# Preparing one quarter of the first batch alone before a recurrence starts

## The chip, the core and the metric

The kernel runs on one core of one Trainium2 chip. The metric is device microseconds of one execution. Five engines work side by side on the core: TensorE (PE in the profile), VectorE (DVE), ScalarE (ACT), GpSimd (POOL) and SyncE (SP, which here only issues transfers). They are joined by semaphores, which the tile framework inserts; each engine takes its own instructions strictly in the order in which they were put in its queue.

## The reference, cut to what matters

The input is `x` of 8 batches x 384 channels x 32 x 32 positions, fp32. Layer 0 is a bidirectional selective scan with a depthwise convolution beside it, layer 1 a causal attention and a quantised feed-forward net. For the change only layer 0 up to its recurrence matters:

```python
xn = rmsnorm(x)                                      # over the 384 channels
u, z = split(xn @ in_proj_w.T)
u = silu(causal_conv1d(u, 4 taps) + bias)            # fwd; on the flipped sequence for bwd
dt, Bm, Cm = split(u @ x_proj_w.T)                   # 24, 16, 16 rows
delta = softplus(dt @ dt_proj_w.T + dt_proj_b)       # [L, 384]
h = exp(delta * A) * h + (delta * u) * Bm            # over L = 1024 positions, 16 states a channel
y = sum(h * Cm, over the 16 states) + u * D
g = (y * silu(z)) @ out_proj_w.T                     # fwd + bwd
x = x + 0.5 * (0.25 * g + sigmoid(depthwise3x3(xn)) * xn)
# layer 1: t = t + attention(layernorm(t)); t = t + bitlinear_ffn(layernorm(t))
```

## The kernel before, in words

Channels lie on the 128 partitions in three chunks `c`, positions along the free axis in two halves `h` of 512. The two directions `d` and two halves make four quarters of a batch, which the recurrence takes in the order `PARTS = ((0,0),(0,1),(1,1),(1,0))` (direction, half): forward first half, forward second half, and then backward from the far end.

**The recurrence** is cut into `Unit`s: a quarter has 24 (3 chunks x 4 groups of 4 states x 2), a batch 96, the kernel 768. One unit is: on POOL one multiply `g = ud * B` (`s_first`, L612), on ACT two exponentials `da` (L625), on DVE two scans of 512 steps (L633), on ACT, in the quarters that open a direction, a copy of the carry (L638), on POOL a second multiply `g * C` (`s_scan`, L639), and on PE four matmuls that sum the states (`s_sum`, L652). `ud` (delta times u) and `dl` (delta) are read from DRAM, each row spread over four partitions (`s_load`, for the unit `AHEAD + 2` = 4 slots on); B and C come from the DRAM tile `rows` (`s_row`).

**The preparation** of a batch is `before_scan`: load `x`, normalise each half (L343), `in_proj` (three matmuls on PE, copy on ACT L359), `conv` (for the first batch a scale on ACT L369, three multiply-adds on DVE L380, bias on ACT L390; for later batches matmuls with diagonal taps), `silus` (L445, between two loads of the activation table), `sum_of_us` (L449), stores of `u` to DRAM, `project` (`xd`, L499 on PE, L510 on ACT, L512 on DVE), the store of the B and C rows (L520), and `delta` (L532 to L548: one matmul, six ACT and four DVE instructions of 128x512, a load of `u` from DRAM and two stores, `sud` and `sdl`). `gates` makes the silu of z and the local 3x3 convolution (L411, on DVE).

**The order.** Each stage is a list of steps with a guessed weight in us (`Steps`; 2.5 if none is given), and `run(a, b)` interleaves lists in proportion to the weights. The batch that comes first has its whole preparation put into the list `begin`, run alone; only its z and `gates` are in `beside`. Then 102 slots of the recurrence (`first`) run with `beside`: the z and gates of batch 0, the whole preparation of batches 1, 2 and 3, and `binarize` of both feed-forward weights. After that attention and feed-forward of batch after batch are interleaved with the remaining units. That order gives each instruction its priority: the framework schedules by a timing model, and an engine with nothing ready of high priority is given later work. So `binarize` stands in `beside` but runs in part during `begin`.

Loads and stores are issued by SP (`load`, L117; `spill`, L130), the constants and `binarize`'s transfers by ACT. Of the tile pools, `big` has 6 buffers of 128x3072 (a batch's `xn`, the diagonal `taps`, pieces of the binarised weights), `mid` has 10 of 128x1024; eight banks of PSUM are shared by tags.

Of the kernel before, what the change touches and what calls it, by code (L numbers as in the profile page):

```python
# [58 lines left out]
def kernel(  # L59
# [258 lines left out]
    def before_scan(b, tags, emit, later=None, diags=None):  # L318
# [8 lines left out]
        @emit  # L327
        def _():

            st["xn"] = btile(f"xn_{b}")  # L330
            load(st["xn"], x[b].rearrange("(c p) l -> p c l", p=P))
            st["xd"] = mtile(f"xd_{b}")

        for h in range(NH):

            @emit
# [78 lines left out]

        def weights_of(c):
# [8 lines left out]
        emit(lambda: weights_of(0))  # L425
        for c in range(NC):

            @emit
            def _(c=c):
                st["up", c] = mtile(f"up_{b}_{c}")  # L430
                for d in range(2):
                    st["u", d, c] = mtile(f"u{d}_{b}_{c}")
                if c + 1 < NC:
                    weights_of(c + 1)

            for i, to in enumerate((emit, emit if later is None else later)):
                for h in range(NH):
                    to(lambda c=c, i=i, h=h: in_proj(c, i, h), 2.6)
            for d in range(2):
                for h in range(NH):  # L440
                    emit(lambda c=c, d=d, h=h: conv(c, d, h), 3.0)
# [5 lines left out]
            def sum_of_us(c=c):  # L447
# [3 lines left out]
                for d in range(2):  # L451
                    spill((b, "u", d, c), st["u", d, c], f"su_{d}_{b}_{c}")
# [27 lines left out]
            def gates_of_us(c=c, silus=silus, sum_of_us=sum_of_us):  # L480
                with tc.high_priority(offset=60):
                    silus([st["u", 0, c], st["u", 1, c]])
# [10 lines left out]
            for h in range(NH):  # L493

                def project(c=c, h=h):
                    xp = bank_of(f"xp_{b}_{c}_{h}")
                    for d in range(2):
                        with at_once(d == 1):
                            mm = nc.tensor.matmul(  # L499
                                out=xp[d * DW : (d + 1) * DW, :],  # L500
                                lhsT=wx[:, c, :],
                                rhs=st["u", d, c][:, half(h)],
                                start=True,
                                stop=True,
                            )
                        if d == 1:
                            pin(mm)
                    xd = st["xd"][:, half(h)]
                    if c == 0:
                        nc.scalar.activation(xd, xp, AF.Identity, bias=onerow)  # L510
                    else:
                        nc.vector.tensor_tensor(xd, xd, xp, ALU.add)  # L512

                emit(project)

        @emit
        def _():
            for d in range(2):
# [724 lines left out]
```

## Time and profile before

| | |
|---|---|
| median of 3 runs | 4453.81 us (4451.62 to 4459.21) |
| profiled execution | 4445.17 us, span 4443.4 us |
| busy: PE, DVE, ACT, POOL | 83%, 76%, 63%, 81% of the span |
| first instruction of the recurrence on POOL | starts at 142.53 us |
| last one ends | 4209.8 us |
| units of the recurrence | 768, of two POOL instructions of 2.37 us each |

The profiled execution lies 8.6 us under the median of the three runs. Busy time is the time in which an engine executes; waiting, issuing of transfers and semaphores are not counted. An L-number is a line of the kernel above.

### The profile page before, as it was taken

How to read it: one execution, taken by the hardware profiler on the slowest of the kernel's cores; microseconds unless marked ns; L12 is line 12 of the kernel's file. 1: busy time of each engine (PE TensorE's matmuls, PEld its weight loads, DVE VectorE, ACT ScalarE, POOL GpSimd, SP SyncE). 2: the span in 40 equal slices, each digit the busy share in tenths (PEclk: the TensorE clock that was granted, in tenths of full speed). 3: DMA queues.
4: the chain of work that ended last, by engine and by line, in shares of the span. 5: the costliest groups of instructions: out<-in, count | busy, mean ns of one | idle time of the engine just before them, and what ended most of it. 6: DMA issues, size and time to landing. Idle time of an engine off the chain costs nothing.

```text
span 4443.4 us, 43447 instructions
## 1 busy us (share of the span) xinstructions
PE 3701.6 (83%) x12522; PEld 1421.4 (32%) x12522; DVE 3385.8 (76%) x4707; ACT 2803.9 (63%) x5383; POOL 3588.3 (81%) x1560
## 2 busy tenths in 40 slices
PE   3587786998889988889988799988999956997799
PEld 1132222333323333233332233322333312332244
DVE  6899999678977789877798867988676766667623
ACT  4767778576764767756677666776665733664334
POOL 0678889888888898799888998889989899889700
PEclk7696887989988999888998899988899877898899
DMA  6645555224363334642344623446332242224200
GB/s 214 242 150 199 189 206 205 102 98 148 123 228 116 102 126 148 208 160 100 110 137 163 212 98 109 154 148 228 103 105 95 78 146 99 95 83 146 84 18 29
DMA packets 327240, 612.01 MB, mean 138 GB/s; under 512 B 33321, under 2 KB 92121, under 8 KB 327001
## 3 DMA queue, kind: packets, MB, share of 16 engines
q1 hardware_dynamic: 317344, 593.09, 38.7%
q10 hardware_dynamic: 9656, 16.15, 1.1%
q8 instruction: 98, 1.61, 0.1%
q14 instruction: 142, 1.16, 0.1%
HBM read 443.45 MB, written 165.68 MB: 137 GB/s over the span
## 4 chain that ended last, share of the span: by engine, by line
PE 49%; DVE 27%; ACT 9%; issue 6%; POOL 5%; DMA 4%; SPq 0%; ACTq 0%; DVEq 0%; POOLq 0%
DVE g L633 13%; PE s L800 8%; PE pt L883 5%; PE qp L740 5%; PE yp L1052 5%; PE av L897 5%; PE y L652 5%; PE op L710 3%; PE in L352 2%; POOL g L612 2%; PE hp L1008 2%; POOL g L639 2%; DVE loc L411 2%; DVE u L380 2%; ACT da L625 2%
## 5 line engine op out<-in xcount | busy, mean ns | idle before, releaser
L612 POOL TENSOR_TENSOR g<-ud,bc 128x1024 f32<-128x1024 f32 x768 | 1820.1, 2370 | 401.8 <-DMA ud<-sud 145.5
L639 POOL TENSOR_TENSOR g<-g,bc 128x1024 f32<-128x1024 f32 x768 | 1816.8, 2366 | 212.8 <-ACT carry L638 113.4
L625 ACT ACTIVATE da<-dl,amat 128x512 f32<-128x512 f32 x1536 | 1054.8, 690 | 806.7 <-DVE g L633 794.1
L633 DVE TENSOR_TENSOR_SCAN g<-da,carry,g 128x512 f32<-128x512 f32 x768 | 942.8, 1267 | 216.4 <-POOL g L612 177.5
L633 DVE TENSOR_TENSOR_SCAN g<-da,g 128x512 f32<-128x512 f32 x768 | 897.9, 1207 | 154.0 <-POOL g L612 99.3
L652 PE MATMUL y<-g,gather 128*32 128x512 f32 x3072 | 470.4, 689 | 145.1 <-POOL g L639 125.3
L800 PE MATMUL s<-k,q 64*128 64x512 f32 (+3 forms) x1152 | 498.9, 618 | 67.9 <-DVE nm L813 65.4
L813 DVE CUSTOM_DVE_ANT_0 pr<-s,cmask 128x512 f32<-128x512 f32 (+3 forms) x576 | 306.2, 550 | 324.0 <-PE s L800 270.0
L1008 PE MATMUL hp<-t,w 128*128 128x512 f32 x720 | 345.7, 626 | 47.2 <-ACT h L1016 31.4
L886 ACT COPY ptn<-pt 128x512 f32<-128x512 f32 (+3 forms) x576 | 263.1, 477 | 187.2 <-PE pt L883 186.0
L1052 PE MATMUL yp<-h,w 128*128 128x512 f32 x720 | 335.5, 621 | 45.2 <-DVE h L1034 40.6
L883 PE MATMUL pt<-ident,pr 128*128 128x128 f32 x1728 | 337.4, 310 | 12.7 <-ACT ptn L886 11.3
L352 PE MATMUL in<-xn,win 128*128 128x512 f32 x576 | 290.6, 649 | 68.8 <-DVE xc L474 18.1
L883 PEld LDWEIGHTS pt<-ident,pr 128*128 128x128 f32 x1728 | 204.8, 151 | 381.2 <-ACT ptn L886 116.7
L411 DVE SCALAR_TENSOR_TENSOR loc<-xn,vec,loc 128x496 f32<-128x496 f32 (+3 forms) x384 | 265.7, 717 | 14.5 <-ACT loc L400 12.6
L833 ACT ACTIVATE pr<-pr,low 128x512 f32<-128x512 f32 (+3 forms) x384 | 241.3, 630 | 48.0 <-DVE low L827 43.7
L897 PE MATMUL av<-ptn,v 128*64 128x512 f32 (+3 forms) x1152 | 268.6, 532 | 2.2 <-ACT ptn L886 2.2
L532 PE MATMUL dp<-xd,wdt 25*128 25x512 f32 x192 | 157.6, 949 | 129.0 <-ACT du L545 105.9
L740 PE MATMUL qp<-t,wqk 128*128 128x512 f32 x576 | 253.6, 596 | 3.4 <-DVE t L313 3.4
L800 PEld LDWEIGHTS s<-k,q 64*128 64x128 f32 x1152 | 167.3, 213 | 265.2 <-DVE nm L813 160.9
L1008 PEld LDWEIGHTS hp<-t,w 128*128 128x128 f32 x720 | 137.3, 198 | 253.3 <-issue 150.9
L1052 PEld LDWEIGHTS yp<-h,w 128*128 128x128 f32 x720 | 139.3, 198 | 246.7 <-issue 181.3
(149 smaller groups left out, 4364.9 us busy)
## 6 DMA issues: line engine op xcount, KB each, us to landing
ud<-sud SPq DMA_DIRECT2D x384, 256.0 KB, 4.3
dl<-sdl SPq DMA_DIRECT2D x384, 256.0 KB, 3.3
bc<-rows SPq DMA_DIRECT2D x256, 256.0 KB, 3.8
t<-st SPq DMA_DIRECT2D x63, 512.0 KB, 6.2
su<-u SPq DMA_DIRECT2D x48, 512.0 KB, 2.9
du<-su SPq DMA_DIRECT2D x96, 256.0 KB, 4.5
sud<-du SPq DMA_DIRECT2D x96, 256.0 KB, 2.9
sdl<-du SPq DMA_DIRECT2D x96, 256.0 KB, 3.5
```

Source lines behind the costliest of these rows:

```text
L352: nc.tensor.matmul(out=mp, lhsT=st["win", c][:, k, i, :], rhs=st["xn"][:, k, half(h)], start=(k == 0), stop=(k == NC - 1),)
L612: pin(nc.gpsimd.tensor_tensor(g, ud, rows_for(u, 0), ALU.mult))
L625: nc.scalar.activation(da, sst["dl", u.b, u.c, u.part, u.q][:, i, :], AF.Exp, scale=amat[:, u.c, k, u.j : u.j + 1],)
L633: nc.vector.tensor_tensor_scan(gi[:, ::step], da[:, ::step], gi[:, ::step], first, ALU.mult, ALU.add)
L639: pin(nc.gpsimd.tensor_tensor(g, g, rows_for(u, 1), ALU.mult))
L652: mm = nc.tensor.matmul(out=y[k * BLK : (k + 1) * BLK, :], lhsT=gather, rhs=pair[k // 2][:, k % 2, :], start=(u.j == u.first_group), stop= ...
L740: nc.tensor.matmul(out=qp, lhsT=st["wqk"][:, c, o : o + P], rhs=st["xn"][:, c, half(h)], start=(c == 0), stop=(c == NC - 1),)
L800: mm = nc.tensor.matmul(out=ss[e][:, : k1 - k0], lhsT=st["q"][rows_of(e), c, chunk(qi)], rhs=st["k"][rows_of(e), c, k0:k1], start=True, st ...
L883: nc.tensor.transpose(pt[:, chunk(i)], pr[:, e, chunk(j % QT)], ident)
L897: mm = nc.tensor.matmul(out=av[rows_of(e), cols], lhsT=st["v"][:, j, hd * HD : (hd + 1) * HD], rhs=st["ptn", j, e][:, cols], start=(j == 0 ...
L1008: nc.tensor.matmul(out=hp, lhsT=st["w1"][:, c, chunk(m % 2)], rhs=st["xn"][:, c, half(h)], start=(c == 0), stop=(c == NC - 1),)
L1052: nc.tensor.matmul(out=yp, lhsT=st["w2", k // 6][:, k % 6, :], rhs=st["h", k // NC][:, k % NC, half(h)], start=(k == 0), stop=(k == NF - 1),)
```

## The change

For the first batch `before_scan` gets a third list of steps, `lead`. What leads up to the deltas of the quarter (direction 0, half 0) goes into it: the load of `x` (now in two transfers, one for each half), the norm of half 0, all three weight loads, `in_proj` and `conv` of that quarter for the three chunks, one group of three silus of 128x512, the store of these u's, their projection (rows of direction 0 alone), the store of their B and C rows, and three `delta` steps. `lead` is run alone. The other three quarters' steps go into `beside`, ahead of everything else that was there; the z and gates of batch 0 follow them (`more`), then the other batches as before. The first batch's `up` and forward `u` live in two `big` buffers in place of six `mid` ones. `project` becomes `project_parts`, which does one direction or both; u and row stores go half by half (`keep_u`, `keep_rows`).

```diff
@@ -315,7 +315,7 @@
                     )
 
 
-    def before_scan(b, tags, emit, later=None, diags=None):
+    def before_scan(b, tags, emit, later=None, diags=None, lead=None):
 
 
         st = {}
@@ -324,16 +324,23 @@
         def bank_of(name):
             return bank(name, next(turns))
 
-        @emit
+        at_half = (emit if lead is None else lead, emit)
+
+        @at_half[0]
         def _():
 
             st["xn"] = btile(f"xn_{b}")
-            load(st["xn"], x[b].rearrange("(c p) l -> p c l", p=P))
+            given = x[b].rearrange("(c p) l -> p c l", p=P)
+            if lead is None:
+                load(st["xn"], given)
+            else:
+                for h in range(NH):
+                    load(st["xn"][:, :, half(h)], given[:, :, half(h)])
             st["xd"] = mtile(f"xd_{b}")
 
         for h in range(NH):
 
-            @emit
+            @at_half[h]
             def _(h=h):
                 sqs = squares(st["xn"], h, f"n0_{b}")
                 ms = mean_of(lambda c: sqs[c], f"ms_{b}_{h}")
@@ -413,6 +420,43 @@
                 )
             return acc
 
+        def project_parts(c, h, parts):
+            xp = bank_of(f"xp_{b}_{c}_{h}_{len(parts)}_{parts[0]}")
+            for d in parts:
+                with at_once(d != parts[0]):
+                    mm = nc.tensor.matmul(
+                        out=xp[d * DW : (d + 1) * DW, :],
+                        lhsT=wx[:, c, :],
+                        rhs=st["u", d, c][:, half(h)],
+                        start=True,
+                        stop=True,
+                    )
+                if d != parts[0]:
+                    pin(mm)
+            rows = slice(parts[0] * DW, (parts[-1] + 1) * DW)
+            xd = st["xd"][rows, half(h)]
+            if c == 0:
+                nc.scalar.activation(xd, xp[rows, :], AF.Identity, bias=onerow[rows, :])
+            else:
+                nc.vector.tensor_tensor(xd, xd, xp[rows, :], ALU.add)
+
+        def keep_u(c, d, h):
+            if (b, "u", d, c) not in spilled:
+                spilled[b, "u", d, c] = dram.tile(
+                    [P, L], F32, name=f"su_{d}_{b}_{c}", tag=f"sp_u_{d}_{c}"
+                )
+            nc.sync.dma_start(out=spilled[b, "u", d, c][:, half(h)], in_=st["u", d, c][:, half(h)])
+
+        def keep_rows(d, h):
+            if (b, "rows", d) not in spilled:
+                spilled[b, "rows", d] = dram.tile(
+                    [2 * NS, L], F32, name=f"rows{d}_{b}", tag=f"rows{d}"
+                )
+            nc.sync.dma_start(
+                out=spilled[b, "rows", d][:, half(h)],
+                in_=st["xd"][d * DW + BC0 : (d + 1) * DW, half(h)],
+            )
+
         def weights_of(c):
             w = mtile(f"win_{b}_{c}", NC * 2 * P).rearrange("p (k i e) -> p k i e", k=NC, i=2)
             for i in range(2):
@@ -422,23 +466,53 @@
                 )
             st["win", c] = w
 
-        emit(lambda: weights_of(0))
+        at_half[0](lambda: weights_of(0))
+        if lead is not None:
+
+            @lead
+            def _():
+                ups, us = btile(f"ups_{b}"), btile(f"us0_{b}")
+                for c in range(NC):
+                    st["up", c], st["u", 0, c] = ups[:, c, :], us[:, c, :]
+                    if c > 0:
+                        weights_of(c)
+
+            for c in range(NC):
+                lead(lambda c=c: in_proj(c, 0, 0), 2.6)
+                lead(lambda c=c: conv(c, 0, 0), 3.0)
+
+            @lead
+            def _():
+                for c in range(NC):
+                    u = st["u", 0, c][:, half(0)]
+                    pin(nc.scalar.activation(u, u, AF.Silu))
+                pin(nc.scalar.preload_act_table_set(LOG_EXP))
+                for c in range(NC):
+                    keep_u(c, 0, 0)
+
+            for c in range(NC):
+                lead(lambda c=c: project_parts(c, 0, (0,)))
+            lead(lambda: keep_rows(0, 0))
+
         for c in range(NC):
 
             @emit
             def _(c=c):
-                st["up", c] = mtile(f"up_{b}_{c}")
-                for d in range(2):
+                if lead is None:
+                    st["up", c] = mtile(f"up_{b}_{c}")
+                for d in range(2) if lead is None else (1,):
                     st["u", d, c] = mtile(f"u{d}_{b}_{c}")
-                if c + 1 < NC:
+                if lead is None and c + 1 < NC:
                     weights_of(c + 1)
 
             for i, to in enumerate((emit, emit if later is None else later)):
                 for h in range(NH):
-                    to(lambda c=c, i=i, h=h: in_proj(c, i, h), 2.6)
+                    if lead is None or (i, h) != (0, 0):
+                        to(lambda c=c, i=i, h=h: in_proj(c, i, h), 2.6)
             for d in range(2):
                 for h in range(NH):
-                    emit(lambda c=c, d=d, h=h: conv(c, d, h), 3.0)
+                    if lead is None or (d, h) != (0, 0):
+                        emit(lambda c=c, d=d, h=h: conv(c, d, h), 3.0)
 
             def silus(ts):
                 for t in ts:
@@ -448,8 +522,12 @@
                 usum = mtile(f"us_{b}_{c}")
                 nc.vector.tensor_tensor(usum, st["u", 0, c], st["u", 1, c], ALU.add)
                 spill((b, "us", c), usum, f"sus_{b}_{c}")
-                for d in range(2):
-                    spill((b, "u", d, c), st["u", d, c], f"su_{d}_{b}_{c}")
+                if lead is None:
+                    for d in range(2):
+                        spill((b, "u", d, c), st["u", d, c], f"su_{d}_{b}_{c}")
+                else:
+                    for d, h in ((0, 1), (1, 1), (1, 0)):
+                        keep_u(c, d, h)
 
 
             def gates(c=c, silus=silus, sum_of_us=sum_of_us):
@@ -479,7 +557,7 @@
 
             def gates_of_us(c=c, silus=silus, sum_of_us=sum_of_us):
                 with tc.high_priority(offset=60):
-                    silus([st["u", 0, c], st["u", 1, c]])
+                    silus([st["u", 0, c] if lead is None else st["u", 0, c][:, half(1)], st["u", 1, c]])
                     pin(nc.scalar.preload_act_table_set(LOG_EXP))
                 sum_of_us()
 
@@ -491,30 +569,15 @@
 
 
             for h in range(NH):
-
-                def project(c=c, h=h):
-                    xp = bank_of(f"xp_{b}_{c}_{h}")
-                    for d in range(2):
-                        with at_once(d == 1):
-                            mm = nc.tensor.matmul(
-                                out=xp[d * DW : (d + 1) * DW, :],
-                                lhsT=wx[:, c, :],
-                                rhs=st["u", d, c][:, half(h)],
-                                start=True,
-                                stop=True,
-                            )
-                        if d == 1:
-                            pin(mm)
-                    xd = st["xd"][:, half(h)]
-                    if c == 0:
-                        nc.scalar.activation(xd, xp, AF.Identity, bias=onerow)
-                    else:
-                        nc.vector.tensor_tensor(xd, xd, xp, ALU.add)
-
-                emit(project)
+                parts = (1,) if lead is not None and h == 0 else (0, 1)
+                emit(lambda c=c, h=h, parts=parts: project_parts(c, h, parts))
 
         @emit
         def _():
+            if lead is not None:
+                for d, h in ((0, 1), (1, 1), (1, 0)):
+                    keep_rows(d, h)
+                return
             for d in range(2):
                 rows = dram.tile([2 * NS, L], F32, name=f"rows{d}_{b}", tag=f"rows{d}")
                 nc.sync.dma_start(out=rows, in_=st["xd"][d * DW + BC0 : (d + 1) * DW, :])
@@ -550,7 +613,8 @@
 
         for d, h in PARTS:
             for c in range(NC):
-                emit(lambda c=c, d=d, h=h: delta(c, d, h), 3.0)
+                to = lead if lead is not None and (d, h) == (0, 0) else emit
+                to(lambda c=c, d=d, h=h: delta(c, d, h), 3.0)
 
 
 
@@ -1153,8 +1217,10 @@
 
     beside = Steps()
     begin = Steps()
-    before_scan(ORDER[0], ("s", "pt"), begin, beside)
+    more = Steps()
+    before_scan(ORDER[0], ("s", "pt"), beside, more, lead=begin)
     run(begin)
+    beside += more
     beside += steps_of(before_scan, ORDER[1], ("s", "pt"), diags=diags)
     beside += steps_of(binarize, w1, w1s, NC, FF, 2, "w1")
     beside += steps_of(binarize, w2, w2s, NF, C, 8, "w2")
```

## The prediction

> **What bounds the kernel now.** The page's busy line comes first, then the table of stretches, cut by me at the first unit (142 us), the start of attention (800), PE's lull (3600 to 3740) and POOL's end (4213).
>
> ```profile
> PE 3701.6 (83%) x12522; PEld 1421.4 (32%) x12522; DVE 3385.8 (76%) x4707; ACT 2803.9 (63%) x5383; POOL 3588.3 (81%) x1560
> ...
> 0.00:24.00 24.00, 6.40 (x11) 2.86 (x12) 1.67 (x9) 5.90 (x10) 8.30 (x24) 1.00 0.79 270
> 24.00:142.00 118.00, 50.46 (x89) 17.02 (x87) 88.01 (x128) 66.63 (x90) 0.00 (x0) 0.65 0.69 247
> 142.00:800.00 658.00, 486.98 (x1248) 165.01 (x1248) 599.92 (x714) 489.93 (x808) 564.69 (x240) 0.79 0.55 191
> 800.00:3600.00 2800.00, 2480.61 (x8746) 963.77 (x8742) 2224.32 (x3152) 1850.16 (x3644) 2459.74 (x1057) 0.90 0.40 136
> 3600.00:3740.00 140.00, 52.98 (x160) 13.65 (x160) 80.75 (x74) 41.32 (x65) 138.48 (x61) 0.58 0.38 130
> ```
>
> After the stretch and its length come PE, PEld, DVE, ACT and POOL busy. POOL does nothing in the first 142 us but 8.3 us of set-up. From there to 3600 it is 86 to 88% busy, and in the lull 99% while PE has 53 of 140 us. So PE has caught up with the recurrence there: attention has about 140 - 53 = 87 us of slack, and POOL sets the end. After its last instruction (4209.8) only some 230 us of attention of the last batch remain. The time is: start of the recurrence, plus 768 units, plus POOL's gaps, plus that tail.
>
> The second reading is what holds POOL back, from its waits over the whole run and those of 142 to 800 us.
>
> ```profile
> POOL g L612 <- DMA ud<-sud: 145.5, 10, 127.3
> POOL g L612 <- PE y L652: 145.2, 72, 7.4
> POOL g L639 <- ACT carry L638: 113.4, 68, 11.4
> POOL g L639 <- DVE g L633: 79.8, 55, 14.5
> ```
>
> The first line holds one wait of 127.3 us: the opening. The others are short waits for PE, ACT and DVE, which were busy with something else when a unit wanted them.
>
> The third is the timeline at the end of the opening. Columns: start, duration, instruction.
>
> ```profile
> 108.56 1.28 DVE L512 TENSOR_TENSOR xd<-xd,xp 128x512 f32<-128x512 f32 x2
> ...
> 118.88 0.68 DVE L544 TENSOR_TENSOR du<-du,dp 128x512 f32<-128x512 f32 x1
> ...
> 120.60 7.86 SPq L117 DMA_DIRECT2D bc<-rows  x3
> ...
> 129.43 0.34 SPq L548 DMA_DIRECT2D sud<-du  x1
> ...
> 142.53 2.35 POOL L612 TENSOR_TENSOR g<-ud,bc 128x1024 f32<-128x1024 f32 x1 [127.34 <-DMA ud<-sud]
> ```
>
> `xd` is complete at 109.9. The first `du` is ready at 119.6, but its store is issued at 129.4, behind loads of B and C rows on SP; two transfers later POOL starts. From `xd` to POOL: 32.6 us.
>
> **What the Trainium skill says.** "Perfetto Trace Analysis", Optimization Strategy, says that a kernel may have several regimes with different most-contended engines, and that interleaving them can pay. The trace agrees on the premise: POOL 0% against DVE 75% in 24 to 142, then POOL 86% but DVE 91%. The second regime has little room on DVE. "DMA: Bandwidth & Descriptors", Anatomy of one DMA, says a transfer's semaphore wait happens on the issuing sequencer, before dispatch; so a waiting store holds up what follows on its queue, as `sud` at 129.4 shows from the other side. "ScalarE: Activation LUTs", What ACT_TABLE_LOAD costs, gives about 1283 ns for a load and 1380 more for a drain; L445's loads take 1283 ns here, and no separate drain shows.
>
> **Part 1: the opening shortens.** The chain for one quarter, from the rows of before. `x` is loaded as now; ACT starts its squares at 16.8, behind constants on its own queue, so splitting that load is costed at nothing, those constants being the cover (without it, one 12 us landing gets a few us shorter). Means of one half, 6 matmul passes instead of 12: end 22.5. Ln and Exp 0.66 + 0.58, three L343 at 0.74: xn ready at 25.9. `in_proj` for three chunks, 6 passes x 0.43 each: 28.5, 31, 33.7. Copy 0.58, scale 0.69, three taps at 0.75, bias 0.69 behind the last: 38; binarize pieces between them as now (L230, 0.6 each): 40. Table load 1.28 and three silus of 512 at an estimated 0.55 (half of 1.05, rounded up): 43. Three projections at about 1 us on a cold PE, overlapping: 44.5; one L510 at 0.69 and two L512 at 0.68: `xd` at 46.5. Then the same 32.6 us: POOL starts at about **79**, 63 us earlier. The SP queue still carries du, bc and sud loads and stores in that stretch; nine fewer deltas could save the 10 us behind bc, six weight loads and three u stores ahead could cost as much. I take 55 to 70.
>
> **Part 2: what is moved has to run beside the recurrence.** Of the opening's 88 us on DVE in 24 to 142, the lead keeps three L343, nine L380, two L512 and twelve delta instructions: 2.2 + 6.7 + 1.4 + 8.3 = 18.6. Moved: L343 3 x 0.74 = 2.2, L380 27 x 0.75 = 20.2, L449 3 x 1.22 = 3.7, L512 4 x 0.68 = 2.7, deltas. Of these before already did five quarter-steps after 142, so four to five of nine count, about 4.5 x 2.8 = 12.6. Sum 41 on DVE. On ACT the same steps: bias and scale 18 x 0.69 = 12.4, copies 1.8, silus 4.8, norm 3.1, deltas 4.5 x 3.7 = 16.7: 39, and one more pair of table loads, 2.6. PE has 171 us idle in 142 to 800 and hides its part (27 cold passes, under 30 us). SP gets about 40 issues of 0.35 to 0.6 us, spread; `ud` has three buffers and is loaded four slots ahead, which covers them unless a store waits long at the head.
>
> In the extreme that DVE is the bound, only its idle time in the opening is gained: 118 - 88 = 30 us before. From 24 to 79 at 80% busy it leaves 11: gain 19. If binarize (L230, L255, L260, L261: 39 us of DVE now done in the opening) finds its `big` buffers held by `up` and `u`, that gain goes to 0. In the other extreme scans go ahead of everything and POOL keeps its 63 us. Against the first extreme: POOL took (658 us for 120 units) 5.48 us a unit with DVE at 91%, and 5.30 (2800 us for 528.5 units) with DVE at 79%. So the beside work of the first stretch costs POOL only about 0.18 x 120 = 22 us. In the steps' weights, that work grows from 616 to 717 (mine, by adding them up: 101 moved), 16%. Proportional: 4 us. With DVE full for as long as the moved work lasts: 41 / 0.91 = 45. I take **26**, near the middle, since DVE has only 58 us idle in that stretch.
>
> **Part 3: what is late next.** Quarter 2 is wanted 24 units after the start: 79 + 24 x 5.5 = 211. On the list its deltas end at weight 83 of 717, slot 12 of 102; its loads come at slot 24. DVE has to do before that: lead 18.6, moved part up to those deltas 37, binarize 39, scans 24 x 2 x 1.24 = 60, in all 155 us; at 90% it is done at 24 + 172 = 196, with two landings of 5 us at 206. It just fits. The attention of batch 0 may begin late by up to 45 us against now; the 87 us of slack cover it.
>
> **Sum.** 4445.2 - 63 + 26 = 4408 for an execution like the profiled one; the median of before lies 8.6 higher, so **4417**, which is 37 us or 0.8% less. About 0.2%, 9 us, is what a measurement of this kernel can tell from no change.
>
> **Rivals.** *POOL keeps the whole shift*: 4454 - 63 + 4 = 4395. For it: short waits and slack on DVE after 800 (79%). Against: DVE at 91%. *DVE takes it back*: gain 0 to 19, so 4435 to 4454. For it: 600 of 658 us busy. Against: the small difference in POOL's pace. *The second quarter comes late*: slower. Place: L612 of unit 24, waiting for `ud`; the work above fits with 5 us to spare, and ACT's silus, stores waiting at SP's head and PSUM banks shared with batch 1 could each add to it. It decides from a stall of 37 us, which eats the gain; a stall of 60 gives 4417 + 60 = 4477, and like delays of the quarters after it could add some more. Against it: the list places those deltas 12 slots, 66 us, early. *It does not do what it says*: the timing model puts binarize or quarters 2 to 4 ahead of the lead, since an idle engine takes what is ready; POOL then starts at 120 or later, and the time is within 10 us of now. Last, any new order changes small waits all through the run; by the unit groups of 24, which take 110 to 140 us here, I allow 15 us either way.
>
> **How the numbers follow.** Forecast 0.42, whole shift 0.10, DVE takes it back 0.18 (half of it under 0.2%), no change in effect 0.04, second quarter late 0.26. Faster: 0.42 + 0.10 + 0.09 = 0.61, less 0.02 for the scatter: 0.59. Same: 0.09 + 0.04 = 0.13. Slower: 0.26 and 0.02: 0.28. The range reaches from the whole shift with some scatter, 4385, to the late quarter's 4477; outside I leave 0.15. The forecast's own range is 4398 to 4440.
>
> **What would show it.** Right: first L612 on POOL at 72 to 90; units 0 to 119 taking 660 to 700 us instead of 658; PE's lull at 3600 shorter by some 35 us; L639's last end near 4173. Wrong: a wait of L612 for `ud` over 20 us near unit 24 (late quarter); first L612 after 110 (no effect); POOL's last end unmoved with DVE above 96% in the first stretch (DVE takes it back). A gain over 60 would mean that the beside work costs nothing.

## The result and the profile after

| | before | after |
|---|---|---|
| median | 4456.51 us (4 runs, 4451.62 to 4467.60) | 4497.49 us (4 runs, 4493.14 to 4500.48) |
| profiled execution, span | 4445.17, 4443.4 us | 4500.05, 4498.3 us |
| first unit on POOL starts | 142.53 us | 71.57 us |
| batch 0, last delta done (DVE, `du`) | 177 us | 243 us |
| batch 1, norm ends (DVE) | 235 us | 309 us |
| batch 0, first attention matmul (PE, `op`) | 768 us | 853 us |
| unit 95 / 239 / 503 / 671 / 767 ends | 681 / 1460 / 2848 / 3716 / 4210 us | 643 / 1496 / 2931 / 3788 / 4265 us |

The changed kernel is slower: the ratio is 1.0089 (95% interval 1.0072 to 1.0106), 41 us by the medians. The forecast was 4417, with a range up to 4477. A lower granted clock of TensorE is not the reason: the two profiles show 0.869 before and 0.859 after, but a kernel below (`e16`) takes 4447 us at 0.859. The two profiled executions differ by 54.9 us: that of before lies 11 us under the median of its runs, that of after 3 us above. The sums below are made between these two.

First the busy line of the page, then the table of stretches of the changed kernel, cut as before (PE, PEld, DVE, ACT, POOL).

```profile
PE 3746.1 (83%) x12522; PEld 1428.8 (32%) x12522; DVE 3411.4 (76%) x4711; ACT 2820.8 (63%) x5394; POOL 3604.8 (80%) x1560
```

```profile
24.00:142.00 118.00, 57.95 (x114) 16.87 (x112) 79.74 (x100) 73.48 (x111) 56.98 (x25) 0.65 0.45 161
142.00:800.00 658.00, 454.23 (x1162) 153.40 (x1162) 603.94 (x689) 461.45 (x733) 529.49 (x222) 0.76 0.56 193
800.00:3600.00 2800.00, 2461.43 (x8418) 946.83 (x8418) 2199.88 (x3106) 1835.00 (x3568) 2389.13 (x1026) 0.89 0.40 136
3600.00:3740.00 140.00, 107.97 (x462) 41.55 (x462) 93.50 (x137) 75.08 (x170) 126.28 (x56) 0.81 0.39 133
```

In the first row POOL has 57 us where it had none. The next two rows take it back: POOL does 35 us less than before in 142 to 800 and 71 us less in 800 to 3600. The last row seems to say that PE's lull is half gone; most of it has only moved, as shown further down.

The timeline around the first unit (start, duration, instruction; in brackets the idle time before it and what ended it):

```profile
46.55 0.67 DVE L441 TENSOR_TENSOR xd<-xd,xp 64x512 f32<-64x512 f32 x1
...
57.60 0.54 SPq L611 DMA_DIRECT2D sud<-du  x1
...
71.57 2.34 POOL L676 TENSOR_TENSOR g<-ud,bc 128x1024 f32<-128x1024 f32 x1 [58.32 <-DMA dl<-sdl]
```

The opening does what it should: POOL starts 71 us earlier. What happened to the 71 us is in the ends of units, the later kernel's against the earlier's: unit 3 is 68 us ahead, unit 95 is 38 us ahead, unit 119 is 14 us ahead; unit 239 is 36 us behind, unit 503 is 83 us behind, and the last one 55 us behind. So **57 us go in the first 120 units, 97 more between units 119 and 503, and 28 come back by the end**: -71 + 57 + 97 - 28 = 55. Of the 57, 33 go in the first 96 units and 24 in the 24 after them.

The waits of POOL over the whole run (us in total, times, longest) show no single large one but the opening:

```profile
POOL g L676 <- PE y L716: 175.5, 67, 17.0
POOL g L703 <- ACT carry L702: 155.8, 81, 13.8
...
POOL g L703 <- DVE g L697: 80.9, 49, 8.8
POOL g L676 <- DMA dl<-sdl: 58.3, 1, 58.3
```

Waits for PE grew from 145 to 175 us and those for the carry from 113 to 156. Between its first and its last unit POOL takes 126 us longer than before; all its waits in that time grew by 110 us, those for ACT by 42, for DVE (counting all its instructions) by 41 and for PE by 32. The only wait for `ud` that a multiply of POOL has in the whole run is of 2.6 us: the second quarter was in time.

### What happens to the first stretch: binarize, and DVE

`binarize` (L230, L255, L260, L261) ran before in the opening, and all its DVE work lay before POOL's first multiply. Now the stretch ahead of POOL is short. ACT's timeline has the transfer of a piece and the first sign, DVE's the last tap of the convolution that reads `ups`.

```profile
53.28 0.40 ACTq L214 DMA_DIRECT2D w<-in_w  x1
...
132.46 2.75 ACT L259 ACTIVATE sg_w<-w 128x3070 f32<-128x3070 f32 x1
```

```profile
129.04 0.73 DVE L387 SCALAR_TENSOR_TENSOR u<-ups,vec,u 128x509 f32<-128x509 f32 x1
```

The first piece has its mean taken off by 65 us, but its sign, which needs a `big` buffer of its own, comes at 132, just after the last reader of `ups` ended at 129.8. That fits a wait for the buffer that `ups` holds; no run isolated it. From 132 on the remaining pieces run beside POOL, where some of DVE's instructions take longer. The groups of DVE in 0 to 330 us (busy us, mean ns, then idle time before them), after and then before:

```profile
L255 DVE TENSOR_SCALAR w<-w,mean_w 128x614 f32<-128x614 f32 (+3 forms) x20 | 20.9, 1100 | 2.3 <-DMA w<-in_w 2.3
L260 DVE TENSOR_TENSOR sg_w<-sg_w,w 128x3070 f32<-128x3070 f32 (+3 forms) x4 | 13.2, 3308 | 2.6 <-ACT sg_w L259 2.6
...
L230 DVE TENSOR_REDUCE sums_w<-w 128x1 f32<-128x614 f32 (+3 forms) x20 | 11.1, 618 | 4.0 <-DMA w<-in_w 4.0
```

```profile
L230 DVE TENSOR_REDUCE sums_w<-w 128x1 f32<-128x614 f32 (+3 forms) x20 | 11.2, 622 | 2.1 <-DMA w<-in_w 2.1
...
L260 DVE TENSOR_TENSOR sg_w<-sg_w,w 128x3070 f32<-128x3070 f32 (+3 forms) x4 | 10.1, 2537 | 0.8 <-ACT sg_w L259 0.8
...
L255 DVE TENSOR_SCALAR w<-w,mean_w 128x614 f32<-128x614 f32 (+3 forms) x20 | 7.8, 453 | 2.9 <-DMA w<-in_w 2.9
```

The same 20 subtractions cost 20.9 instead of 7.8 us (the long ones are seven that run beside POOL's multiplies), while the reductions cost the same, though ten of them run beside POOL. The Trainium skill, "SBUF — State Buffer", Who interferes with whom, describes this: VectorE and GpSimd share a pair of ports, and whichever issues first holds it for its whole instruction. `tensor_scalar` can enter a two-port form that needs the pair, a `tensor_tensor` with both inputs in SBUF contends with a GpSimd instruction that reads SBUF, and `tensor_reduce` doesn't contend on trn2. The trace agrees in each of the three, and the loss falls on POOL too:

```profile
198.13 4.89 DVE L260 TENSOR_TENSOR sg_w<-sg_w,w 128x3040 f32<-128x3040 f32 x1
```

```profile
199.79 5.43 POOL L676 TENSOR_TENSOR g<-ud,bc 128x1024 f32<-128x1024 f32 x1
```

That multiply normally takes 2.35 us. With the rest of binarize and the sum of u's (L523), stretched in the same way, DVE has some 19 us more to do than before.

The rest of the delay is scans: until the last delta of batch 0 is done, DVE had done 14 of them in the old order (17 us) and does 52 in the new one (63 us), 46 us more. 46 + 19 is about the 66 us by which that delta is later. In 142 to 240 us (after, then before) DVE has next to nothing to give:

```profile
142.00:240.00 98.00, 33.54 (x82) 8.79 (x82) 97.94 (x101) 55.22 (x96) 72.63 (x28) 0.53 0.74 258
```

```profile
142.00:240.00 98.00, 51.70 (x117) 17.43 (x118) 92.91 (x120) 77.75 (x131) 82.16 (x36) 0.71 0.51 184
```

DVE is 97.94 of 98 us busy (92.91 before), and all preparations that follow are late by the same amount: batch 1 by 74, batch 2 by 77, batch 3 by 76, the attention of batch 0 by 81 to 86.

### Where the other 97 us go: the recurrence is pulled back to attention's place

From unit 119 on (792 us) binarize is long done, and still the recurrence falls from 14 us ahead to 83 behind, about where attention is (75 us behind for batch 3, by the end of its `op`). In the eight kernels below whose slots are not moved, unit 503 lies within 29 us of that place too, though it ranges from 15 us early to 82 late. The order of instructions is a written one, with so many units between so many steps of attention, and each engine takes its queue strictly in order. One place where it shows: PE and then POOL of the changed kernel around 1951 us.

```profile
1935.63 7.03 PE L1116 MATMUL yp<-h,w 128*128 128x512 f32 x16
1942.59 1.12 PE L595 MATMUL dp<-xd,wdt 25*128 25x512 f32 x2
1943.64 4.56 PE L1116 MATMUL yp<-h,w 128*128 128x512 f32 x10
1948.13 1.98 PE L595 MATMUL dp<-xd,wdt 25*128 25x512 f32 x4
1950.04 1.92 PE L716 MATMUL y<-g,gather 128*32 128x512 f32 x16
```

```profile
1951.56 2.36 POOL L676 TENSOR_TENSOR g<-ud,bc 128x1024 f32<-128x1024 f32 x1 [9.58 <-PE y L716]
```

PE works almost without a break, through feed-forward and deltas that stand before the sums of the units in its queue; then two pairs of units' sums (16 matmuls) come at once, and POOL has waited 9.58 us for a buffer of `g`. A wait "for PE" is here a wait for other work on PE.

What PE's lull near 3600 us waits for is read from these stretches, first before, then after:

```profile
3600.00:3660.00 60.00, 17.21 (x56) 4.06 (x60) 34.30 (x30) 17.45 (x26) 59.63 (x26) 0.53 0.39 141
3660.00:3740.00 80.00, 35.77 (x109) 9.59 (x108) 46.45 (x44) 23.86 (x40) 78.85 (x35) 0.62 0.36 122
3740.00:3800.00 60.00, 59.31 (x185) 25.60 (x188) 36.80 (x38) 32.87 (x67) 56.07 (x25) 1.00 0.21 74
```

```profile
3600.00:3660.00 60.00, 56.44 (x246) 22.64 (x247) 43.42 (x89) 43.50 (x116) 51.71 (x23) 0.83 0.24 84
3660.00:3740.00 80.00, 51.53 (x218) 18.92 (x216) 50.07 (x48) 31.59 (x56) 74.57 (x33) 0.80 0.49 171
3740.00:3800.00 60.00, 17.69 (x56) 3.85 (x57) 33.51 (x30) 18.36 (x30) 60.00 (x27) 0.53 0.35 112
```

PE's emptiest stretch (17 of 60 us busy) stands at 3600 before and at 3740 after. It is attention of batch 6 waiting for its own last gates, which the recurrence delivers:

```profile
3652.47 7.54 PE L710 MATMUL op<-gy,wout 128*128 128x512 f32 x12 [9.29 <-DMA gy<-sgy]
```

```profile
3723.61 7.93 PE L774 MATMUL op<-gy,wout 128*128 128x512 f32 x12 [9.28 <-DMA gy<-sgy]
```

These two matmuls are 71 us apart, as are the ends of unit 671 (71.5): the lull ends with the recurrence and can absorb nothing of the recurrence's own lateness. What it does absorb is lateness of attention: `op` is about 100 us late for batch 5, ahead of the lull, and 72 for batch 6, at its end. In every kernel of this study the last `op` matmul of batch 6 ends 18 to 20 us after unit 671. In the best kernel below (`e13`) PE is idle for 38 us of 3600 to 3800, against 88 before and 74 after.

### The profile page after: what moved, and what is told of

It is laid out like the page before. It is cut to its first block, busy times and chain, and to the rows that moved or that the text cites. A ratio compares the mean times of both kernels' runs of the same rounds, so it can differ in the third digit from the quotient of the medians.

```text
span 4498.3 us, 43476 instructions
## 1 busy us (share of the span) xinstructions
PE 3746.1 (83%) x12522; PEld 1428.8 (32%) x12522; DVE 3411.4 (76%) x4711; ACT 2820.8 (63%) x5394; POOL 3604.8 (80%) x1560
## 4 chain that ended last, share of the span: by engine, by line
PE 51%; DVE 28%; ACT 9%; issue 7%; POOL 3%; DMA 2%; SPq 0%; ACTq 0%; DVEq 0%; POOLq 0%
DVE g L697 13%; PE s L864 8%; PE yp L1116 6%; PE qp L804 6%; PE pt L947 5%; PE y L716 5%; PE av L961 5%; DVE loc L418 3%; PE in L359 3%; PE ap L1014 2%; PE vp L822 2%; DVE u L387 2%; PE op L774 2%; PE hp L1072 2%; ACT da L689 2%
## 5 line engine op out<-in xcount | busy, mean ns | idle before, releaser
L676 POOL TENSOR_TENSOR g<-ud,bc 128x1024 f32<-128x1024 f32 x768 | 1835.6, 2390 | 396.5 <-PE y L716 175.5
L703 POOL TENSOR_TENSOR g<-g,bc 128x1024 f32<-128x1024 f32 x768 | 1822.2, 2373 | 258.6 <-ACT carry L702 155.8
L716 PE MATMUL y<-g,gather 128*32 128x512 f32 x3072 | 496.9, 708 | 168.1 <-POOL g L703 156.8
L864 PE MATMUL s<-k,q 64*128 64x512 f32 (+3 forms) x1152 | 508.7, 621 | 73.1 <-DVE nm L877 71.5
L716 PEld LDWEIGHTS y<-g,gather 128*32 128x32 f32 x3072 | 66.6, 115 | 475.6 <-POOL g L703 254.6
```

The costliest lines, as they stand in the source:

```text
L676: pin(nc.gpsimd.tensor_tensor(g, ud, rows_for(u, 0), ALU.mult))
L703: pin(nc.gpsimd.tensor_tensor(g, g, rows_for(u, 1), ALU.mult))
L716: mm = nc.tensor.matmul(out=y[k * BLK : (k + 1) * BLK, :], lhsT=gather, rhs=pair[k // 2][:, k % 2, :], start=(u.j == u.first_group), stop= ...
L864: mm = nc.tensor.matmul(out=ss[e][:, : k1 - k0], lhsT=st["q"][rows_of(e), c, chunk(qi)], rhs=st["k"][rows_of(e), c, k0:k1], start=True, st ...
```

## The experiments

Theory L: the new start is lost because the rest of the preparation, with binarize displaced into it, comes late on a full DVE, and the recurrence's lead is not kept by the written order. Rivals: the place of the three quarters in the list (a wait for them), or DVE's load alone. All ratios are to before on the same chip, with 95% intervals. Ends of units and `op` (the last of those matmuls of batch 0) are from one profile each, us against before.

| kernel | us | ratio | batch 1's norm | `op` | unit 95 | unit 503 | unit 767 |
|---|---|---|---|---|---|---|---|
| after | 4497 | 1.0089 [1.0072, 1.0106] | +74 | +81 | -38 | +83 | +55 |
| `e1_rest_first` | 4512 | 1.0133 [1.0091, 1.0174] | +78 | +84 | -35 | +86 | +65 |
| `e2_after_nobin` | 4465 | 1.0016 [1.0005, 1.0028] | +17 | +4 | -89 | -1 | +4 |
| `e3_before_nobin` | 4437 | 0.9954 [0.9942, 0.9965] | -9 | -19 | -34 | +1 | +1 |
| `e4_bin_early` | 4459 | 0.9996 [0.9986, 1.0005] | +48 | +48 | -52 | +9 | +20 |
| `e9_after_binlate` | 4485 | 1.0067 [1.0040, 1.0095] | +17 | +21 | -88 | +53 | +52 |
| `e10_before_binlate` | 4452 | 0.9990 [0.9978, 1.0002] | -9 | -18 | -32 | +26 | +2 |
| `e14_before_binheld` | 4485 | 1.0071 [1.0045, 1.0097] | +53 | +44 | +2 | +44 | +31 |
| `e15_after_fewtaps` | 4487 | 1.0070 [1.0047, 1.0093] | +62 | +33 | -31 | +34 | +39 |
| `e5_after_shift` | 4465 | 1.0011 [0.9998, 1.0023] | +77 | +69 | -37 | +6 | +15 |
| `e6_before_shift` | 4435 | 0.9950 [0.9935, 0.9964] | +1 | -1 | +6 | -9 | -9 |
| `e11_binearly_shift` | 4433 | 0.9950 [0.9930, 0.9970] | +45 | +45 | -53 | -17 | -16 |
| `e12_before_shift24` | 4448 | 0.9977 [0.9966, 0.9989] | +5 | +1 | -9 | -14 | +5 |
| `e13_binearly_shift24` | 4423 | 0.9922 [0.9905, 0.9940] | +46 | +43 | -53 | -27 | -24 |
| `e16_after_shift24` | 4448 | 0.9975 [0.9963, 0.9988] | +74 | +64 | -42 | -17 | +4 |
| `e17_binearly_shift36` | 4433 | 0.9942 [0.9921, 0.9963] | +46 | +60 | -53 | -25 | -10 |

**Is it the place of the three quarters?** `e1_rest_first` puts them into a list that is run ahead of the recurrence's slots.

```diff
-    before_scan(ORDER[0], ("s", "pt"), beside, more, lead=begin)
+    rest_0 = Steps()
+    before_scan(ORDER[0], ("s", "pt"), rest_0, more, lead=begin)
     run(begin)
+    run(rest_0)
```

> The changed kernel, but the three other quarters of batch 0 stand in the order ahead of the recurrence's slots again (own list, run between the lead and the first stretch); only z and gates stay beside. Theory L (the written order and the preparation list set the pace; a recurrence that is ahead of its place in the order does not stay ahead): batch 0's deltas are complete near 170 instead of 235, the norm of batch 1 comes near 235 instead of 302, the first output-projection matmul of attention near 770 to 790 instead of 855, and the time falls to 4435 to 4465. Theory P (POOL sets the end, its start counts): POOL starts later than in the changed kernel or is held back, and the time stays at 4490 or rises. Theory C (the loss is binarize's DVE work beside a busy POOL): depends on where binarize lands; if it stays after 130 us, 4480 to 4500.

It changed next to nothing: every position lies within 5 us of after up to unit 671, and it is no quicker. Theory L's expectation of it (4435 to 4465) missed; 4512 is what theory P expected, though the start on POOL moved by 3 us only. That the scheduler gives an idle engine what is ready, so that the same scans run beside the same steps, would explain it. The place in the list isn't the cause.

**Is it binarize?** `e2` and `e3` leave it out, in the changed kernel and in the old one (the feed-forward reads the raw weights).

```diff
-    w1s = dram.tile([C, FF], F32, name="w1s", tag="w1s", bufs=1)
-    w2s = dram.tile([FF, C], F32, name="w2s", tag="w2s", bufs=1)
+    w1s, w2s = w1, w2
...
-    beside += steps_of(binarize, w1, w1s, NC, FF, 2, "w1")
-    beside += steps_of(binarize, w2, w2s, NF, C, 8, "w2")
```

> The changed kernel without the binarization of the two feed-forward weights (the raw weights are read in its place). Theory C: the loss against the same cut of the kernel before (the next run) shrinks from 41 to under 15 us. Theory L: it stays at 30 us or more, since the scans that moved in between the preparation's steps are still there; only the 20 us of stretched DVE instructions go.

> The kernel before without the binarization of the two feed-forward weights (the raw weights are read in its place): the pair of the run above. The opening loses 39 us of DVE work that filled gaps: the start of the recurrence moves from 142 to about 115 to 130, and the time falls by 10 to 30 us by every theory.

Binarize makes batch 1's norm 9 us late in the old kernel and 74 - 17 = 57 in the new one: most of the 74 is binarize. But the change still costs 4465 - 4437 = 28 us with no binarize in either, between what theory C (under 15) and theory L (30 or more) had said and near the latter. (Their profiled executions, 4450.2 and 4446.7, differ by only 3.5 us: the one lies 15 us under the median of its 12 runs, the other 10 us above that of its 20. The medians count.) `e2` also shows the second loss alone: its recurrence is 89 us ahead at unit 95 and still 60 at 239, its attention is 21 us late at most, and at unit 503 the lead is 1 us. That no lead goes in its first 96 units, where after loses 33, shows that those 33 are binarize's. A start 55 us earlier than `e3`'s (61.3 against 116.6) brought nothing at the end.

**Does binarize's place mend it?** `e4` runs both right after the lead; `e9` and `e10` spread them over the attention of batch 0.

```diff
     run(begin)
+    run(steps_of(binarize, w1, w1s, NC, FF, 2, "w1"))
+    run(steps_of(binarize, w2, w2s, NF, C, 8, "w2"))
```

> The changed kernel with both binarizations placed in the order right after the lead, ahead of the recurrence and of the other three quarters. Theory C: most of the binarize pieces (subtract of 128x614 at 0.53 us free, 2.2 us beside POOL) run before POOL starts or have the buffers in time, and the time falls by 20 to 30 us to 4467 to 4477. Theory L: the other quarters are later still, so no gain: 4490 to 4520. Rival on the buffers (two of six big buffers held by up and u stop binarize from 65 to 132 us): binarize still stops there whatever its place, and nothing moves by more than 10 us.

`e4` gains 39 us on after, more than theory C had said. POOL starts 7 us later (78.5), and L255 takes 12.8 us in all: two of the four pieces have it done by then, the other two, at 116 and 150, still meet POOL's multiplies. `ups` and the forward u's hold two `big` buffers here as well, so these alone don't stop binarize.

```diff
+        att = steps_of(attention, b, fed) if i < B - 1 else []
+        if i == 0:
+            binar = steps_of(binarize, w1, w1s, NC, FF, 2, "w1")
+            binar += steps_of(binarize, w2, w2s, NF, C, 8, "w2")
+            att = spread_over(att, binar)
+        rest += att
-        rest += steps_of(attention, b, fed) if i < B - 1 else []
```

> The changed kernel with binarize taken out of the first stretch and spread over the attention of batch 0, where DVE is 64 to 70% busy. If the loss is binarize's DVE work (39 us, and 19 us of stretching beside POOL) pushed into the stretch that DVE bounds, then batch 1's norm comes at about +17 against before as in the run without binarize, attention of batch 0 at 0 to +10, and the time falls to 4455 to 4475. If binarize disturbs attention as much there, the time stays over 4485.

> The kernel before with binarize spread over the attention of batch 0: the control of the run above. Without binarize that kernel had its second batch 9 us earlier and ended 0.5% earlier by the median. If binarize is hidden in the opening's gaps there, moving it brings no gain: 4440 to 4465.

`e9` has its first stretch mended (norm +17, as without binarize), and then pays in the attention of batch 0: `op` of batch 0 is 21 late (0 to 10 were expected), that of batch 1 64, and the time is 10 us over what was expected of a cure. Against the same kernel without binarize (`e2` or `e3`), binarize costs 32 us where the change leaves it, 20 in the attention of batch 0 and nothing right after the lead (4459 against 4465). The old kernel did not have it for nothing either: 22 us in the opening, where it delays the start (142.5 against 116.6), and 15 in the attention of batch 0.

`e14` is the converse: the old kernel with nothing of the change but a binarize that can't begin before the recurrence does (a tiny copy from the first unit's carry stands ahead of each piece's load).

```diff
+            carry = sst["carry", ORDER[0], 0, 0]
+            nc.vector.tensor_copy(v[:, 0, 0:1], carry[:, 0, 0, 0:1])
             nc.scalar.dma_start(out=v, in_=part(src, k, n))
```

> The kernel before, with one thing of the change alone: binarize is pushed into the recurrence. A 128x1 copy from the first unit's carry into each weight tile stands ahead of its load, so no load of binarize can start before the first unit has run (about 150 us). Nothing of batch 0's preparation is moved. Theory D (DVE work displaced into the stretch that DVE bounds, and stretched beside POOL): the opening gets 5 to 20 us shorter, the subtractions of 128x608 rise from 0.53 to 1 to 2.5 us each, batch 1's norm comes 25 to 55 us later than in the kernel before, and the time is 4470 to 4500. If the binarize pieces are not the cause: within 10 us of 4459.

The kernel is 26 us slower than before, with batch 1's norm 53 us late. Its first unit starts at 111 us, 31 us earlier than before (5 to 20 were expected); that lead is gone by unit 23, which is 9 us late. Its groups of DVE in 0 to 330 us (L257 and L262 are the L255 and L260 of the others):

```profile
L257 DVE TENSOR_SCALAR w<-w,mean_w 128x614 f32<-128x614 f32 (+3 forms) x20 | 18.9, 999 | 1.9 <-DMA w<-in_w 1.9
...
L262 DVE TENSOR_TENSOR sg_w<-sg_w,w 128x3070 f32<-128x3070 f32 (+3 forms) x4 | 13.6, 3411 | 0.0
```

The stretching is about the same without the change: it comes from running beside POOL.

**Is it the order?** `e5` and `e6` put 12 more slots of the recurrence beside the first preparation and move every due time of attention by 12 units; nothing else. `e12` and `e16` do the same with 24, in the old kernel and in the changed one.

```diff
-    first = slots(-AHEAD - 2, per + 2)
-    others = slots(per + 2, len(units) + 2)
+    first = slots(-AHEAD - 2, per + 2 + 12)
+    others = slots(per + 2 + 12, len(units) + 2)
...
-            due.append((sum(us for _, us in rest), i * per))
+            due.append((sum(us for _, us in rest), i * per - 12))
```

> The changed kernel with 12 more of the recurrence's 768 slots put beside the first stretch, and all later slots 12 places earlier against attention: the written order itself gives the recurrence a lead of about 64 us. The runs so far show a recurrence that is up to 91 us ahead (without binarize) lose all of it by unit 500. Theory L (order): the loss stops earlier, the recurrence ends up some 40 to 60 us earlier at unit 500 than in the changed kernel (+83 against before becomes +20 to +40), attention stays 70 to 100 late, PE's lull at 3600 goes, and the time is 4450 to 4480. Theory R (the engines: PE and DVE have no room for a recurrence that runs ahead): unit 500 stays at +70 or more and the time within 10 us of 4497.

> The kernel before with the same 12 slots, the control of the run above. Theory L: the recurrence is ahead by 20 to 50 us at unit 500, PE's lull at 3600 (87 us idle) shrinks, time 4415 to 4445. Theory R: no change at unit 500, time within 10 us of 4457; attention may come later by what the scans take.

> The kernel before with 24 slots moved forward. Twelve gave 24 us. Theory L: PE's lull at 3600 still had 80 us idle with twelve, so more is to be had: 4415 to 4435. Theory R (DVE in the first stretch is full, extra units there delay batches 1 to 3): attention of batch 0 comes 15 us or more later, and the time is 4435 to 4460.

> The changed kernel with 24 slots moved forward and binarize left where the change has it. Twelve gave -33 us. If only the order is wrong in the change, 24 should bring it near the kernel before with 12, 4435 to 4450. If the displaced binarize costs its own 20 to 30 us whatever the order: 4450 to 4465.

The order decides how much of the lead is lost. With the same opening and nearly the same late attention (`op` +69 and +64), the loss between units 95 and 119 goes from 24 us to 1, that between 119 and 503 from 97 to 42 (12 slots) and 24 (24 slots), and the time from 4497 to 4465 and 4448. After unit 503 `e16` loses some more (+12 at unit 671). In 160 to 2850 us POOL's waits for PE and for the carry, 141.4 and 115.7 us in after, become in `e16`:

```profile
POOL g L676 <- PE y L716: 119.8, 56, 15.3
POOL g L703 <- ACT carry L702: 76.3, 46, 10.7
```

The old kernel had an order that was not quite its best either (12 slots: -24 us, as theory L said, though the lead at unit 503 is 9 us and not 20 to 50), but 24 slots are worse than 12 for it, while the changed one still gains. Both theories of `e12` missed: the time is theory R's, but attention is only 1 us late. So the gain of the slots is not all a mending of the change: against the old kernel with as many slots, the change costs 41 us with none, 30 with 12 and nothing with 24, and best against best (4448 and 4435) it still costs 12.

**Both together.** `e11`, `e13` and `e17` are `e4` with 12, 24 and 36 slots.

> The changed kernel with binarize right after the lead and 12 recurrence slots moved forward. Each alone gave about -35 us against the changed kernel (4459 and 4465). Theory L and D together: they act on different terms (when attention starts, and how far the recurrence may run ahead of it), so they add in part: 4425 to 4445, beside 4435 of the kernel before with the 12 slots alone. If both act on the same slack: 4455 to 4465.

> The changed kernel with binarize right after the lead and 24 slots moved forward. The recurrence starts 60 to 70 us earlier here, 12 slots' time, so if the order should follow the start, 24 here do what 12 do in the kernel before: 4420 to 4440. If the first stretch's DVE is the limit: no better than with 12.

> The changed kernel with binarize right after the lead and 36 slots moved forward; 0, 12, 24 gave 4459, 4433, 4423. With the recurrence limited by the order alone it gains 5 to 10 us more: 4410 to 4420. With DVE full in the first stretch, attention starts later than with 24 and it is at 4425 to 4445.

| slots moved | 0 | 12 | 24 | 36 |
|---|---|---|---|---|
| before | 4457 | 4435 | 4448 | |
| after | 4497 | 4465 | 4448 | |
| after, binarize early | 4459 | 4433 | **4423** | 4433 |

With 36 slots (`e17`) the gain shrinks, and attention is later than with 24 (+60 against +43), as expected for a full DVE. `e13` beats both kernels: 0.9922 [0.9905, 0.9940], 36 us less than before on its chip (4458.9) and 75 less than after. Against the old opening in its own best order of those tried (4435) it is 13 us less, with intervals that just overlap (0.9935 to 0.9964 there).

**Is it DVE's load?** `e15` leaves the four corner taps out of the local convolution of batches 0 to 3 in the changed kernel; that is 96 multiply-adds (4 taps x 3 chunks x 2 halves x 4 batches), some 68 us of DVE in the first stretch.

```diff
-                if k == 4:
+                if k == 4 or (b in ORDER[:4] and k in (0, 2, 6, 8)):
                     continue
```

> The changed kernel with the four corner taps of the local 3x3 convolution left out for batches 0 to 3: 4 taps x 6 halves x 4 batches x 0.7 us = 68 us less DVE work in the first stretch, and nothing else changed. If DVE bounds that stretch and its preparation list decides when attention begins: the first output-projection matmul comes 50 to 70 us earlier than the changed kernel's 855 (at 785 to 805), and the time falls to 4440 to 4470. If something else holds the list (ACT, PSUM banks, the order of scans): it comes less than 25 us earlier and the time stays over 4480.

```profile
142.00:800.00 658.00, 464.41 (x1188) 157.36 (x1180) 555.12 (x628) 469.20 (x771) 530.71 (x222) 0.76 0.59 203
```

DVE falls from 604 to 555 us here, and POOL does as much as in after (530.7 against 529.5). `op` of batch 0 comes 48 us earlier: so DVE's work is what makes preparation and attention late. But the kernel is only 11 us quicker than after (the intervals overlap), where 27 to 57 were expected if that were all. The recurrence is again pulled to where attention is (+34 at unit 503), and the 28 us that after gets back by the end do not come back here (+34 to +39). Why after regains them and `e15` doesn't, no run settles.

## Why the prediction was wrong

- **Part 1 was right, with a better size.** 63 us were forecast (55 to 70), 71 came, just over the range. `xd` was ready at 47.2 (46.5 forecast); from there it took 24 us instead of 32.6, because `sud` went out at 57.6, a microsecond after its `du`, and not 10 us behind loads of rows. That was named as the possible saving.
- **The step that failed first: "POOL sets the end", with "87 us of slack" in attention that "cover it".** PE's 53 of 140 us in the lull were read as slack against anything late. They are a wait for the recurrence: attention of batch 6 is done with all but its own gates. Slack of that kind covers a late attention while the recurrence keeps its time (28 us were so covered), and the recurrence didn't: it shares PE, ACT and DVE with attention in one written order, and by unit 503 it had lost its lead and 83 us more. This loss of 97 us between units 119 and 503 stood in the sum at nothing. `e5` and `e16` cut it to 42 and 24 with the order alone; `e2` shows a lead of 89 us lost with attention 21 us late at most.
- **The second: Part 2's cost to POOL, 26 us (4 to 45), was 57** for the first 120 units, which took 720 us (71.6 to 791.9) instead of the forecast 660 to 700. The text had the cause in hand, binarize that finds its `big` buffers held, but priced it as lost room in the opening (gain 0). It missed that the same instructions take longer beside POOL (+19 us on DVE with the sum of u's) and that the scans of the early units take DVE from what prepares batches 1 to 3. The first 96 units lose 33 us with binarize and none without (`e2`); the other 24, in units 96 to 119, are again the order's (1 in `e5` and `e16`). `e14` prices binarize's displacement at 26 us of the end.
- **Part 3.** Quarter 2 was in time, as forecast: the only wait for `ud` is of 2.6 us. The attention of batch 0 was to be late by up to 45 us, and was late by 81 to 86.
- **The signs to watch.** First L676 at 72 to 90: 71.6. Lull shorter by 35: PE's idle time in 3600 to 3860 fell from 94 to 75 us, and the end of the lull moved by 71. Last L703 near 4173: 4264.8.
- **The rivals.** The late second quarter had the sign, not the mechanism. "DVE takes it back" (gain 0 to 19) had the mechanism of the first loss, DVE full at 97.94 of 98 us, though it is full only in places (92% over the stretch); it did not foresee a loss. It is near what remains once order and binarize are mended, 13 us, which may be chance. None of the signs named for being wrong came: each looked for one place or one full engine, and the loss is spread over some two hundred waits of about 2.1 us each, where before had as many of 1.7.

## What to carry to other kernels

Where two streams share in-order queues in a written order, an earlier start of one is worth something only if the order is moved with it: look at the position of each stream along the run (ends of units, first matmuls of each batch), and try a few places. Before calling an idle stretch slack, ask what ends it, and whether that would be late too. Work that fills an opening is not free to move: ask where it goes, and price it at its duration beside the engine that runs there. When an order is tuned for the new kernel, tune it for the old one too, or the gain of the tuning is taken for a gain of the change.

## What was not expected of the hardware

- A 128x608 subtraction on DVE takes 0.52 us alone and 2.17 on the mean of three beside POOL's multiplies (2.62 at most), which fits a wait for a whole POOL instruction of 2.35 us. A reduction of the same tile takes 0.77 either way. Scans that read `da` from PSUM take 1.21 either way, and multiply-adds of the convolution into PSUM (L387) 0.75.
- A 128x1024 sum of two SBUF tiles (L523) takes 1.22 us alone, and up to 8.7 beside POOL, in both kernels (before it is L449). POOL pays in its turn: 5.43 instead of 2.35 us behind one DVE instruction of 4.89.
